# Attention with a mixture of experts: transposes by halves and the causal mask in the tiling of the scores

## The chip, the cores and the metric

The kernel runs on one core of a Trainium2 chip. The metric is the device time of one execution in microseconds. A core has TensorE (PE in the profile, its weight loads PEld), VectorE (DVE), ScalarE (ACT), GpSimd (POOL) and SyncE (SP, which here issues most DMAs). Each works through its own list of instructions in order, and semaphores tie them together.

## The reference

One layer on x of 8 x 1024 x 512 floats. Attention has 16 heads of 32 features. Queries, keys and values are no projections: each is the sine and cosine of an angle.

```python
theta_q = xh / (1.0 + jnp.abs(w_q)) + b_q + t * phi_q
Q = jnp.concatenate([cos_q, sin_q], axis=-1)          # K likewise
V = cos_v + sin_v
scores = jnp.einsum('bqhd,bkhd->bhqk', Q, K) / scale
scores = jnp.where(causal, -jnp.inf, scores)          # keys after the query
attn = jax.nn.softmax(scores, axis=-1)
out = jnp.einsum('bhqk,bkhd->bqhd', attn, V).reshape(B, S, D)
theta_out = out / (1.0 + jnp.abs(w_out)) + b_out       # then cos + sin
```

Then x = x + attention(layernorm(x)), and x = x + ffn(layernorm(x)). The ffn is a mixture of 8 experts, two for each token, each expert with room for 160 tokens of a sequence; an expert is 512 to 2048 to 512 with a relu.

## The kernel before

The attention comes first, up to about 1476 us, then the experts. All of it is in fp32.

Attention goes through 32 steps n, one for each sequence b and chunk c of four heads (128 features). Four heads are two pairs pr; the two heads of a pair lie in partitions 0 to 63 and 64 to 127 of a qk tile, cosine and sine together being 64 features. The index a is the head within a pair.

scores (L574) computes, for a pair and a half h of 512 queries, blocks of 128 keys against the queries that may see them. Each score tile holds two PSUM banks, one for each head. The two matmuls of a block use 64 rows of the array each ("64*128" in the profile), and run side by side. Half 0 has three tiles (512 columns; 384 + 128; 256), half 1 seven (five of 512; 384 + 128; 256). A profile line counts an fp32 matmul twice, since it is two passes. ScalarE takes Exp of a tile into an e tile in SBUF (L580). In the three tiles of each half that hold blocks on the diagonal, VectorE multiplies the diagonal blocks by seen, a matrix of ones and zeros (L590). attend (L604) multiplies e by the values: 128 rows, 64 columns for each head ("128*64"), all blocks added in one PSUM bank av. VectorE takes av out to av_sb with a factor (L611). turn transposes av_sb in four 128 x 128 transposes (L641, "128*128"), and VectorE divides by the sum that came along as a 33rd value (L644, L646).

qk_pre does the transposes of the normalized input for the next but one step (L458, then L463 on VectorE), eight for a step. qk_abs, square, sine and qk_sin are ScalarE's part of sine and cosine (L474, L399, L402, L482). qk_post multiplies on VectorE (L405) and rearranges through eight DMAs. v_pre, v_post make the values, o_pre, o_post the output angle. ScalarE loads a table before the sines and another before the next Exp.

The router of sequence b - 1 begins at the end of step c = 0 of the next sequence: statistics and a root on VectorE, then for each tile of 128 tokens rows (L679, normalized, sent off by DMA), features (four transposes, L691, and a copy, L692), parts (L698, "128*32") and whole (L710). Later parts choose experts and places.

The order on TensorE, VectorE and ScalarE is written out by hand, as the program emits it. Generators yield after each tile; run goes round its generators, two tiles each in turn, and steps the asides (qk_abs, v_pre, layernorm1, the router) after each turn. So score tiles and products alternate in short runs:

```python
av11, e01 = run(
    attend(n - 1, 1, 1, e11) if late else iter(()), scores(pairs[0], 1),
    aside=asides,
)
```

[...] ps_sc has two score tiles (four banks), ps_av two, ps_tr two of one bank for all transposes and the router's matmuls. In the experts' stage ps_p takes the six that the first two held.

Of the kernel before, what the change touches and what calls it, by code (L numbers as in the profile page):

```python
# [11 lines left out]
F32 = mybir.dt.float32  # L12
# [54 lines left out]

ROOT_GUESS = float(0x5F3759DF)
# [3 lines left out]
def preln_attn_moe_kernel(  # L72
# [61 lines left out]
    avp = to_router.pool("avp", 2, **left)  # L134
# [52 lines left out]
    ps_tr = to_end.pool("ps_tr", 2, space=PSUM)  # L187
# [12 lines left out]
    ps = ps_tr.tile([P, 6 * NCH], F32, name="ps_t")  # L200
# [24 lines left out]
    seen = own.tile([P, P], F32, name="seen")  # L225
# [17 lines left out]

    def rest_of_loads():

        for op, t in ((ALU.is_ge, seen), (ALU.is_gt, before)):
            nc.gpsimd.affine_select(
                out=t, in_=ones, compare_op=op, fill=0.0, base=0, pattern=[[1, P]],
                channel_multiplier=-1,
            )  # L250
        nc.gpsimd.iota(
# [48 lines left out]
    ps_sc = to_pairs.pool("ps_sc", 2, space=PSUM)  # L300
# [27 lines left out]
    def load_b1():  # L328
        t = own.tile([E * NHC, P], F32, name="vec_in")
        nc.sync.dma_start(t, b1.rearrange("e (c p) -> (e c) p", p=P))  # L330
        ps = ps_tr.tile([P, P], F32, name="ps_t")
# [7 lines left out]
    def load_mid(b):  # L339
# [6 lines left out]
        st = small.tile([P, NTT, NCH, nc.vector.BN_STATS_DIM], F32, name="st_mid")  # L346
# [101 lines left out]
    def qk_pre(n):  # L448
# [5 lines left out]
        for h in range(2):  # L454
            yield
            ps = ps_tr.tile([P, 4, P], F32, name="ps_t")
            for t in range(4):
                nc.tensor.transpose(  # L458
                    ps[:, t, :], xn_tiles[b][h][:, t, c * P : (c + 1) * P], ident
                )  # L460
            for i in range(2):
                cols = (slice(None), i, slice(512 * h, 512 * (h + 1)))
                nc.vector.scalar_tensor_tensor(  # L463
                    p[cols], ps.rearrange("p t q -> p (t q)"),
                    inv_qk[:, i * NCH + c : i * NCH + c + 1], base[cols], ALU.mult, ALU.add,
                )
        yield p, r
# [97 lines left out]
    def scores(pair, h):  # L565

        es = []
        for parts in tiles_of(h):
            n = sum(w for _, _, w, _ in parts)
            ps = ps_sc.tile([P, 2, 512], F32, name="ps_s")  # L570
            for kb, q0, w, at in parts:
                for a in range(2):
# [3 lines left out]
                        rhs=pair[r, 0, q0 : q0 + w], start=True, stop=True,  # L576
                    )

# [4 lines left out]
            if parts[0][0] >= 4 * h:  # L583

                if len(parts) == 1:
                    own_keys, k = e[:, :, :P], seen.unsqueeze(1).to_broadcast([P, 2, P])
# [7 lines left out]
    def attend(n, pr, h, es):  # L594
# [4 lines left out]
        for i, parts in enumerate(tiles):  # L599
            if i:  # L600
                yield
# [12 lines left out]
    def run(*gens, aside=()):  # L614
# [3 lines left out]
        while live:  # L618
            for i in list(live):
# [7 lines left out]
                for g in aside:  # L627
                    next(g, None)
# [666 lines left out]
```

## Time and profile before

| | |
|---|---|
| median of 3 runs | 3486.86 us (3486.4 to 3488.84) |
| the profiled execution | 3486.65 us, span 3484.9 us |
| TensorE busy | 3302.9 us (95%) |
| VectorE busy | 2469.3 us (71%) |
| ScalarE busy | 1315.7 us (38%) |
| granted TensorE clock | 0.992 |

The span runs from the first to the last instruction of the profiled execution. Matmul starts are recorded, their ends are modelled, so busy time of TensorE overlaps between neighbours, and a gap between two runs is read from start to start. In the groups a line names the code line, engine, operation and tiles, then its count, busy time, mean duration in ns, and the idle time of the engine before it with what ended it. x3072 of L574 is 1536 matmuls of two passes.

### The profile page before, as it was taken

The page shows a single profiled execution, that of the slowest core. Times are in us where ns is not written, and L with a number is a line of the kernel's source. Part 1 is how long each engine was busy: PE and PEld are TensorE (multiplying, and loading weights), DVE is VectorE, ACT ScalarE, POOL GpSimd, SP SyncE. Part 2 cuts the span into 40 slices and gives each one's busy share as a digit, 9 for nine tenths or more (in the row PEclk, how much of TensorE's full clock was granted, in tenths as well). Part 3 has the DMA queues.
Part 4 walks back from the last instruction along what each step waited for, and adds up shares of the span by engine and source line. Part 5 has one row for each costly group of instructions (what it writes and reads, how often), then busy time and mean ns, then how long its engine had stood idle before and what let it go on. Part 6 is the DMA issues. An engine that isn't in the chain of part 4 may idle for free.

```text
span 3484.9 us, 43387 instructions
## 1 busy us (share of the span) xinstructions
PE 3302.9 (95%) x15974; PEld 2171.9 (62%) x15974; DVE 2469.3 (71%) x5569; ACT 1315.7 (38%) x1609; POOL 391.1 (11%) x346
## 2 busy tenths in 40 slices
PE   3899999999999999889999999999999999999998
PEld 1344444444444444458868868778778688688687
DVE  7897989898989878574684585576566747746844
ACT  5676767676767676420120111111111101101201
POOL 0000202020202020232101101100110111011010
PEclk9999999999999999999999999999999999999999
DMA  4434343434353434142232322422322323322321
GB/s 142 125 93 148 90 154 91 154 91 153 91 178 89 132 87 135 46 137 39 75 106 46 112 61 49 112 55 61 106 46 67 103 43 76 103 38 76 105 40 25
DMA packets 242684, 320.45 MB, mean 92 GB/s; under 512 B 30312, under 2 KB 163112, under 8 KB 230056
## 3 DMA queue, kind: packets, MB, share of 16 engines
q1 hardware_dynamic: 220304, 275.54, 26.7%
q0 software_dynamic: 22080, 42.10, 6.8%
q8 instruction: 127, 2.08, 0.2%
q14 instruction: 85, 0.70, 0.1%
q10 hardware_dynamic: 88, 0.02, 0.0%
HBM read 188.67 MB, written 61.82 MB: 72 GB/s over the span
## 4 chain that ended last, share of the span: by engine, by line
PE 79%; DVE 12%; ACT 5%; issue 2%; DMA 1%; POOL 0%; POOLq 0%; DVEq 0%; ACTq 0%; SPq 0%
PE ps_p L1010 27%; PE ps_p L965 24%; PE av L604 11%; PE ps_s L574 11%; ACT e L580 4%; PE ps_t L641 2%; DVE e L590 1%; PE ps_t L921 1%; PE ps_t L458 1%; PE ps_t L691 1%; DVE qk_c L405 1%; DVE av_sb L611 1%; DVE qk_r L405 1%; DVE xn L679 0%; PE ps_t L698 0%
## 5 line engine op out<-in xcount | busy, mean ns | idle before, releaser
L580 ACT ACTIVATE e<-ps_s 128x1024 f32<-128x1024 f32 (+1 forms) x640 | 564.5, 937 | 389.8 <-PE ps_s L574 385.9
L574 PE MATMUL ps_s<-qk 64*128 64x512 f32 (+3 forms) x3072 | 607.7, 512 | 62.0 <-ACT e L580 40.4
L1010 PE MATMUL ps_p<-w,hid 128*128 128x256 f32 x2560 | 569.4, 380 | 0.0
L604 PE MATMUL av<-e,v 128*64 128x512 f32 (+3 forms) x3072 | 557.4, 499 | 5.8 <-DVE e L590 5.8
L1010 PEld LDWEIGHTS ps_p<-w,hid 128*128 128x128 f32 x2560 | 484.5, 190 | 66.3
L574 PEld LDWEIGHTS ps_s<-qk 64*128 64x128 f32 x3072 | 277.9, 187 | 326.1 <-issue 160.2
L1010 PE MATMUL ps_p<-w_t,hid 128*128 128x256 f32 x1920 | 430.5, 379 | 1.3 <-DVE w_t L886 1.3
L604 PEld LDWEIGHTS av<-e,v 128*64 128x64 f32 x3072 | 195.5, 138 | 322.1 <-issue 264.2
L1010 PEld LDWEIGHTS ps_p<-w_t,hid 128*128 128x128 f32 x1920 | 361.7, 190 | 49.7 <-DVE w_t L886 2.1
L965 PE MATMUL ps_p<-xe_s,t 128*128 128x256 f32 (+1 forms) x1024 | 299.8, 436 | 3.4 <-DVE t L950 3.4
L965 PE MATMUL ps_p<-xe,w 128*128 128x256 f32 (+1 forms) x1024 | 298.3, 434 | 0.2
L965 PE MATMUL ps_p<-xe,t 128*128 128x256 f32 (+1 forms) x1024 | 296.8, 433 | 0.0
L657 POOL DMA_INDIRECT slot_d<-token,slot x128 | 149.4, 1167 | 1146.9 <-issue 636.9
L590 DVE TENSOR_TENSOR e<-e,seen 128x256 f32<-128x256 f32 (+1 forms) x384 | 184.4, 510 | 118.3 <-ACT e L580 115.1
L965 PEld LDWEIGHTS ps_p<-xe_s,t 128*128 128x128 f32 x1024 | 194.6, 191 | 87.3 <-DVE t L950 7.9
L1039 ACT COPY p<-ps_p 128x256 f32<-128x256 f32 x40 | 14.7, 368 | 612.5 <-PE ps_p L1010 612.5
L965 PEld LDWEIGHTS ps_p<-xe,t 128*128 128x128 f32 x1024 | 194.4, 190 | 80.5
L965 PEld LDWEIGHTS ps_p<-xe,w 128*128 128x128 f32 x1024 | 192.8, 190 | 82.5 <-DVE hid L983 5.9
L1032 POOL DMA_INDIRECT out_dram<-y,slots x80 | 126.4, 1580 | 671.5 <-DVE y L1027 528.6
L914 POOL DMA_INDIRECT xg<-xn_d,source x80 | 78.3, 979 | 1026.8 <-PE ps_t L921 1017.1
L922 DVE COPY xe<-ps_t 128x512 f32<-128x512 f32 x80 | 55.3, 691 | 194.9 <-PE ps_t L921 194.3
L980 ACT ACTIVATE p<-ps_p,b_t 128x256 f32<-128x256 f32 (+1 forms) x128 | 65.5, 512 | 330.5 <-DVE y L1026 170.0
(193 smaller groups left out, 3874.0 us busy)
## 6 DMA issues: line engine op xcount, KB each, us to landing
w<-in_L_ffn_W_dram SPq DMA_DIRECT2D x256, 256.0 KB, 3.2
qk<-qk_c SPq DMA_DIRECT2D x128, 256.0 KB, 4.5
qk<-qk_r SPq DMA_DIRECT2D x128, 256.0 KB, 4.6
w<-in_L_ffn_W_dram SPq DMA_DIRECT2D x64, 512.0 KB, 7.1
qk_base<-base_d SPq DMA_DIRECT2D x29, 1024.0 KB, 5.1
xn_d<-xn SPq DMA_DIRECT2D x72, 256.0 KB, 2.0
x_mid<-in_L_attn_x_dram SPq DMA_DIRECT2D x16, 1024.0 KB, 8.5
out_dram<-x_mid SPq DMA_DIRECT2D x8, 2048.0 KB, 11.7
```

The lines of the kernel that those rows point to most:

```text
L405: nc.vector.scalar_tensor_tensor(out, f.bitcast(F32), LIFT, s, ALU.add, ALU.mult)
L574: nc.tensor.matmul(ps[:, a, at : at + w], lhsT=pair[r, 1, kb * P : (kb + 1) * P], rhs=pair[r, 0, q0 : q0 + w], start=True, stop=True,)
L580: nc.scalar.activation(e, ps[:, :, :n], AF.Exp, scale=UNIT * UNIT / math.sqrt(2 * DH))
L590: nc.vector.tensor_tensor(own_keys, own_keys, k, ALU.mult)
L604: nc.tensor.matmul(av[a * 64 : (a + 1) * 64, q0 - 512 * h :], lhsT=vt[:, kb, 2 * pr + a, :], rhs=es[i][:, a, at : at + w], start=kb == 0, ...
L641: nc.tensor.transpose(ps[:, t, :], av_sb[:, t * P : (t + 1) * P], ident)
L657: nc.gpsimd.indirect_dma_start(out=slot_d[b], out_offset=bass.IndirectOffsetOnAxis(ap=idx, axis=0), in_=src, in_offset=None,)
L914: nc.gpsimd.indirect_dma_start(out=xg, out_offset=None, in_=xn2_d[i % 2], in_offset=bass.IndirectOffsetOnAxis(ap=source[:, e, j0 + j, None ...
L965: nc.tensor.matmul(ps, lhsT=weights[:, k, :], rhs=rows[:, k, :], start=k == 0, stop=k == 1)
L980: nc.scalar.activation(p1, product(b11, a11), AF.Identity, bias=b1_t[:, e * NHC + q : e * NHC + q + 1])
L1010: nc.tensor.matmul(ps, lhsT=hs[k][:, part, cols], rhs=ws[k][weight], start=k == 0, stop=k == NHQ - 1,)
L1032: nc.gpsimd.indirect_dma_start(out=out, out_offset=bass.IndirectOffsetOnAxis(ap=meta[:, e, jj[r], 0:1], axis=0), in_=ys[r], in_offset=None ...
```

## The change

Transposes go by halves: by_halves transposes the upper and the lower 64 rows of a block apart, each into one bank of a tile, in the tiling of the scores. The tiles come from ps_sc, which now has three of two banks; ps_tr is gone until the experts' stage. qk_pre, turn and features each fill one such tile with eight blocks, and VectorE reads it with other strides. turn is called once for both halves of a pair.

The mask is added to the scores before Exp: bf16 matmuls of keys_b (an identity, shifted by part) with later_b (0 or -FAR) add onto the diagonal blocks, four for each of those tiles. VectorE's multiplication is gone.

The order is new. some steps generators a given number of tiles; a step goes in runs of three to five tiles of scores or products, with transposes next to scores; the ten score tiles of a pair follow each other, both halves in one list. The router's rows and features come in twos. The e tiles keep their number; avp has three buffers.

```diff
+FAR = 1000.0 * math.sqrt(2 * DH) / (UNIT * UNIT)
...
+    ps_sc = to_pairs.pool("ps_sc", 3, space=PSUM)
+    def two_banks():
+        return ps_sc.tile([P, 2, 512], F32, name="ps_s")
+    def by_halves(turned, src):
+        for a in range(2):
+            r = slice(a * 64, (a + 1) * 64)
+            nc.tensor.transpose(turned[:, a, :], src[r, :], ident[r, r])
...
-    seen = own.tile([P, P], F32, name="seen")
+    keys_b = own.tile([P, 2, P], BF16, name="keys_b")
+    nc.vector.memset(keys_b, 0.0)
+    later_b = own.tile([P, 2, P], BF16, name="later_b")
...
+    later = row2.tile([P, NCH, 2 * P], F32, name="xT", bufs=1)[:, :3, :P]
+    def mask():
+        for part in range(2):
+            for a in range(2):
+                r = slice(a * 64, (a + 1) * 64)
+                nc.vector.tensor_copy(later_b[r, part, :], later[r, 1 + part - a, :])
+                nc.vector.tensor_copy(keys_b[r, part, part * 64 : part * 64 + 64], ident[r, r])
...
-        for h in range(2):
-            yield
-            ps = ps_tr.tile([P, 4, P], F32, name="ps_t")
-            for t in range(4):
-                nc.tensor.transpose(
-                    ps[:, t, :], xn_tiles[b][h][:, t, c * P : (c + 1) * P], ident
+        ps = two_banks()
+        for t in range(NTT):
+            by_halves(
+                ps[:, :, t * 64 : (t + 1) * 64],
+                xn_tiles[b][t // 4][:, t % 4, c * P : (c + 1) * P],
+            )
+        for i in range(2):
+            for a in range(2):
+                cols = lambda t: t[:, i, :].rearrange("p (t a q) -> p t a q", a=2, q=64)[:, :, a, :]
+                nc.vector.scalar_tensor_tensor(
+                    cols(p), ps[:, a, :].rearrange("p (t q) -> p t q", q=64),
+                    inv_qk[:, i * NCH + c : i * NCH + c + 1], cols(base), ALU.mult, ALU.add,
                 )
-            for i in range(2):
-                cols = (slice(None), i, slice(512 * h, 512 * (h + 1)))
-                nc.vector.scalar_tensor_tensor(
-                    p[cols], ps.rearrange("p t q -> p (t q)"),
-                    inv_qk[:, i * NCH + c : i * NCH + c + 1], base[cols], ALU.mult, ALU.add,
-                )
-        yield p, r
+            yield p, r
...
-    def scores(pair, h):
-        es = []
+    def scores(pair, h, es):
         for parts in tiles_of(h):
             n = sum(w for _, _, w, _ in parts)
-            ps = ps_sc.tile([P, 2, 512], F32, name="ps_s")
+            ps = two_banks()
+            own_keys = parts[0][0] >= 4 * h
             for kb, q0, w, at in parts:
                 for a in range(2):
                     r = slice(a * 64, (a + 1) * 64)
                     nc.tensor.matmul(
                         ps[:, a, at : at + w], lhsT=pair[r, 1, kb * P : (kb + 1) * P],
-                        rhs=pair[r, 0, q0 : q0 + w], start=True, stop=True,
+                        rhs=pair[r, 0, q0 : q0 + w], start=at == 0, stop=not own_keys,
+                        skip_group_check=True,
                     )
+            if own_keys:
+                for part, w in ((0, 64), (1, P)):
+                    for a in range(2):
+                        r = slice(a * 64, (a + 1) * 64)
+                        out_, late = ps[:, a, :w], later_b[r, part, :w]
+                        if len(parts) == 2:
+                            out_ = ps[:, a, :].rearrange("p (k q) -> p k q", q=P)[:, ::3, :w]
+                            late = late.unsqueeze(1).to_broadcast([64, 2, w])
+                        nc.tensor.matmul(
+                            out_, lhsT=keys_b[r, part, :], rhs=late,
+                            start=False, stop=part == 1, skip_group_check=True,
+                        )
             e = ep.tile([P, 2, n], F32, name=f"e_{n}", bufs=8 if n == 512 else 2)
             nc.scalar.activation(
                 e, ps[:, :, :n], AF.Exp, scale=UNIT * UNIT / math.sqrt(2 * DH)
             )
-            if parts[0][0] >= 4 * h:
-                if len(parts) == 1:
-                    own_keys, k = e[:, :, :P], seen.unsqueeze(1).to_broadcast([P, 2, P])
-                else:
-                    own_keys = e.rearrange("p a (k q) -> p a k q", q=P)[:, :, ::3, :]
-                    k = seen.unsqueeze(1).unsqueeze(1).to_broadcast([P, 2, 2, P])
-                nc.vector.tensor_tensor(own_keys, own_keys, k, ALU.mult)
             es.append(e)
-            yield es
-    def attend(n, pr, h, es):
+            yield
+    def attend(n, pr, h, es, halves):
         vt = v_tiles[n % 2]
         av = ps_av.tile([P, 512], F32, name="av")
         tiles = tiles_of(h)
         for i, parts in enumerate(tiles):
-            if i:
-                yield
             for kb, q0, w, at in parts:
                 for a in range(2):
                     nc.tensor.matmul(
...
+            if i + 1 == len(tiles):
+                av_sb = avp.tile([P, 512], F32, name="av_sb")
+                q = 2 * (n % NCH) + pr
+                nc.vector.tensor_scalar(av_sb, av, inv_o[:, q : q + 1], None, ALU.mult)
+                halves.append(av_sb)
+            yield
+    def some(count, *gens):
+        for gen in gens:
+            while count and next(gen, 0) is None:
+                count -= 1
...
-    def turn(pr, h, av_sb, p):
-        ps = ps_tr.tile([P, 4, P], F32, name="ps_t")
-        for t in range(4):
-            nc.tensor.transpose(ps[:, t, :], av_sb[:, t * P : (t + 1) * P], ident)
-        av = ps.rearrange("p t (a f) -> p t a f", a=2)
-        rec = small.tile([P, 4, 2, 1], F32, name="rec")
+    def turn(pr, halves, p):
+        ps = two_banks()
+        for t in range(NTT):
+            by_halves(
+                ps[:, :, t * 64 : (t + 1) * 64],
+                halves[t // 4][:, t % 4 * P : (t % 4 + 1) * P],
+            )
+        av = ps.rearrange("p a (t f) -> p t a f", f=64)
+        rec = small.tile([P, NTT, 2, 1], F32, name="rec")
         nc.vector.reciprocal(rec, av[:, :, :, DH : DH + 1])
         dst = p.rearrange("p (t a d) -> p t a d", a=HPC, d=DH)
         nc.vector.tensor_tensor(
-            dst[:, 4 * h : 4 * h + 4, 2 * pr : 2 * pr + 2, :], av[:, :, :, :DH],
-            rec.to_broadcast([P, 4, 2, DH]), ALU.mult,
+            dst[:, :, 2 * pr : 2 * pr + 2, :], av[:, :, :, :DH],
+            rec.to_broadcast([P, NTT, 2, DH]), ALU.mult,
...
+        def features(xns):
+            xT = row2.tile([P, NCH, 2 * P], F32, name="xT", bufs=1)
+            if b == B - 1:
+                for i, xn in enumerate(xns):
+                    ps = pools["ps_tr"].tile([P, NCH, P], F32, name="ps_t")
+                    for c in range(NCH):
+                        nc.tensor.transpose(ps[:, c, :], xn[:, c * P : (c + 1) * P], ident)
+                    copy(xT[:, :, i * P : (i + 1) * P], ps)
+                    yield xT
+            else:
+                ps = two_banks()
+                for i, xn in enumerate(xns):
+                    for c in range(NCH):
+                        at = (NCH * i + c) * 64
+                        by_halves(ps[:, :, at : at + 64], xn[:, c * P : (c + 1) * P])
+                for a in range(2):
+                    copy(
+                        xT.rearrange("p c (i a q) -> p i c a q", a=2, q=64)[:, :, :, a, :],
+                        ps[:, a, :].rearrange("p (i c q) -> p i c q", i=2, q=64),
+                    )
+                yield xT
...
-        ahead = rows(0)
+        ahead = [rows(0), rows(1)]
         yield "tiles"
-        lg, xT_ = None, None
+        lg, xT = None, None
         for g in range(NTT // 2):
             if g:
-                lg = parts(xT_)
-            xT_ = row2.tile([P, NCH, 2 * P], F32, name="xT", bufs=1)
-            for i in range(2):
-                xn = ahead
-                if 2 * g + i + 1 < NTT:
-                    ahead = rows(2 * g + i + 1)
-                features(xn, xT_, i)
-                if i == 0:
-                    yield
+                lg = parts(xT)
+            for xT in features(ahead):
+                yield
+            if g + 1 < NTT // 2:
+                ahead = [rows(2 * g + 2), rows(2 * g + 3)]
             if g:
                 whole(g - 1, lg)
             yield
         yield "sums"
-        lg = parts(xT_)
+        lg = parts(xT)
...
+    mask()
...
+        es, halves = [[], []], [[], []]
+        products = [attend(n, 0, h, es[h], halves[0]) for h in range(2)]
+        if late:
+            products.insert(0, attend(n - 1, 1, 1, e11, halves1))
+        ahead = [scores(pairs[0], h, es[h]) for h in range(2)]
+        places, v_box = [None], [None]
+        absolutes = keep(places, qk_abs(qk_st)) if more else iter(())
+        asides = [keep(v_box, v_pre(n + 1))] if more else [first_rows]
         if route is not None and c > 0:
             asides.append(part(route))
-        if not more:
-            asides.append(first_rows)
...
-        av11, e01 = run(
-            attend(n - 1, 1, 1, e11) if late else iter(()), scores(pairs[0], 1),
-            aside=asides,
-        )
+        def with_asides(count):
+            for _ in range(count):
+                some(1, *ahead)
+                for g in asides:
+                    next(g, None)
+        if late:
+            some(3, *products)
+        if n == 0:
+            with_asides(3)
+            qk_st = rest(qk_pre(1))
+            angle(*qk_st)
+            absolutes = keep(places, qk_abs(qk_st))
+            with_asides(2)
+        else:
+            with_asides(5)
+        some(2, absolutes)
+        if late:
+            some(3, *products)
+        with_asides(4)
+        some(2, absolutes)
+        some(3, *products)
+        with_asides(1)
+        rest(absolutes)
         for g in asides:
             rest(g)
+        if n == 1:
+            load_mid(0)
+        if late:
+            turn(1, halves1, pos)
+            o_st = o_pre(n - 1, pos)
...
+        some(NTT + 2, *products)
         if more:
             v_post(n + 1, v_st)
         if n == 0:
             load_base(2)
-        (e10,) = run(scores(pairs[1], 0))
-        turn(0, 1, av01, pos_n)
+        es, halves1 = [[], []], []
+        ahead = [scores(pairs[1], h, es[h]) for h in range(2)]
+        asides = []
+        if route is not None and c > 0:
+            asides.append(part(route))
+        with_asides(5)
+        turn(0, halves[0], pos_n)
         if late:
             square(o_st[0])
             o_post(n - 1, o_st)
-        places = [None]
-        asides = [keep(places, qk_pre(n + 2))] if n + 2 < NCK else []
-        if route is not None and c > 0:
-            asides.append(part(route))
-        e11, av10 = run(scores(pairs[1], 1), attend(n, 1, 0, e10), aside=asides)
+        some(3, attend(n, 1, 0, es[0], halves1))
+        with_asides(5)
+        if n + 2 < NCK:
+            qk_st = rest(qk_pre(n + 2))
...
+        last = (es[1], halves1, pos_n)
         pairs = next_pairs if more else None
-    turn(1, 0, av10, pos_n)
-    (av11,) = run(attend(NCK - 1, 1, 1, e11))
-    turn(1, 1, av11, pos_n)
+    rest(attend(NCK - 1, 1, 1, es[1], halves1))
+    turn(1, halves1, pos_n)
     to_pairs.close()
```

The hunks left out give parts, whole, places and the first gathers tiles from ps_sc in place of ps_tr (in the last sequence and in the experts' stage a new ps_tr serves), and build later on GpSimd.

## The prediction

> **What bounds the kernel now.** I read the page first (its busy times, then its costliest groups), then TensorE's timeline of one attention step, the list of waits between 100 and 1450 us, and ScalarE's timeline of the same step.
>
> From the page:
> ```profile
> PE 3302.9 (95%) x15974; PEld 2171.9 (62%) x15974; DVE 2469.3 (71%) x5569; ACT 1315.7 (38%) x1609; POOL 391.1 (11%) x346
> ...
> L580 ACT ACTIVATE e<-ps_s 128x1024 f32<-128x1024 f32 (+1 forms) x640 | 564.5, 937 | 389.8 <-PE ps_s L574 385.9
> ...
> L604 PE MATMUL av<-e,v 128*64 128x512 f32 (+3 forms) x3072 | 557.4, 499 | 5.8 <-DVE e L590 5.8
> ...
> L590 DVE TENSOR_TENSOR e<-e,seen 128x256 f32<-128x256 f32 (+1 forms) x384 | 184.4, 510 | 118.3 <-ACT e L580 115.1
> ```
> TensorE is the bound. The masking on VectorE (L590) keeps VectorE busy 184 us, yet TensorE waited for it 5.8 us in all (the idle column of L604): taking it away buys almost nothing on the path by itself.
>
> TensorE's timeline of an attention step without router work (start, duration, instructions, idle before):
> ```profile
> 728.57 5.81 PE L604 MATMUL av<-e,v 128*64 128x512 f32 x32
> 734.30 0.66 PE L641 MATMUL ps_t<-ident,av_sb 128*128 128x128 f32 x4
> 734.89 2.00 PE L574 MATMUL ps_s<-qk 64*128 64x512 f32 x12
> 737.17 0.70 PE L574 MATMUL ps_s<-qk 64*128 64x256 f32 x4 [0.28 <-ACT e L580]
> 737.80 0.66 PE L641 MATMUL ps_t<-ident,av_sb 128*128 128x128 f32 x4
> 738.39 1.99 PE L574 MATMUL ps_s<-qk 64*128 64x512 f32 x8
> 740.30 1.94 PE L604 MATMUL av<-e,v 128*64 128x512 f32 x12
> 742.18 0.66 PE L458 MATMUL ps_t<-ident,xn 128*128 128x128 f32 x4
> ```
> Starts are exact, ends are modelled, so I use starts. 3328 columns of L604 take 5.73 us (728.57 to 734.30), 1024 columns 1.88 (740.30 to 742.18): 1.67 ns a column plus **0.16 us for each run**. Scores of 1024 columns take 1.91 (738.39 to 740.30): 0.20 us a run. Four transposes take 0.59: 0.11 each, and 0.15 for the run. So each change of tiling (64*128, 128*64, 128*128) costs 0.15 to 0.20 us that the busy time hides. Such a step holds 22 runs and lasts 39.6 us (712.41 to 752.03, turn to turn).
>
> Who waits:
> ```profile
> PE ps_s L574 <- ACT e L580: 32.6, 123, 0.3
> ...
> PE ps_t L691 <- DVE xn L679: 15.7, 14, 1.2
> ...
> PE ps_t L698 <- DVE xT L692: 12.0, 14, 1.5
> ```
> The 0.2 to 0.3 us waits recur four times a step: two score tiles are all that PSUM has room for, and the third waits for Exp. The router's waits for VectorE come in one step of four.
>
> The view of av_sb gives the attention's length:
> ```profile
> L611 DVE TENSOR_SCALAR av_sb<-av,inv_o x128: 730/743/752, 78.1 to 1468.8; 128x512 f32<-128x512 f32 x128
> ```
> 127 intervals of 10.95 us, so 43.8 us for each of 32 steps, 1402 us in all. **Ledger before:** scores and products 32 x 18,432 columns x 1.67 ns = 985; 1016 transposes x 0.1075 = 109; router matmuls about 27; 793 runs in the order (254 of scores x 0.20, 539 x 0.16) = 137. Sum 1258, so 144 us are waits.
>
> **What the Trainium skill says.** "TensorEngine Tiling (Array Packing)", Key Properties: changing the tiling mode drains TensorE, changing the tile within a mode doesn't. The trace agrees: 0.15 to 0.20 us at each change, none inside a run. Same page, Gotcha 1: different row tiles must write different PSUM banks; that is why a tile of halves needs two banks. "TensorE: Matmul & The Clock Gate", LDWEIGHTS: columns / 1.2 ns whatever the rows, 107 ns for 128 columns; the trace's 0.11 us for each fp32 transpose agrees. Same page, Weight-path perf modes: 128 non-fp32 weights load about twice as fast; the trace has no bf16 matmul, so nothing here shows it.
>
> **The change, part by part.**
>
> *Runs.* The order of TensorE's instructions has 447 runs instead of 793 (223 in the 64*128 tiling, 224 others): 223 x 0.20 + 224 x 0.16 = 80. Gain **57 us**.
>
> *Transposes by halves.* 1016 transposes become 1016 pairs. A half loads 64x128 weights and streams 64 columns. The two loads are in different rows and go side by side; next load beside this stream: 107 ns a pair, as before, **0**. If load and stream don't overlap it is 107 + 53 = 160 ns: +53. I take 0.
>
> *Masks.* 384 score tiles get four bf16 loads and four matmuls (64 and 128 columns, twice that in the two-block tiles). The first pair of loads hides behind the scores; the second load and the next fp32 load show: 54 + 107 to 107 + 107 ns. I take 0.19 us: **+73**. Lower end 0.12 (+46). The trace before doesn't show bf16 between fp32; if that costs as much as a tiling change on the way in and out, 0.5 (+192).
>
> *VectorE.* 184 us of L590 go; two divisions of 256 elements become one of 512. Worth the 5.8 us above, counted with the waits. The eight small copies of mask() and POOL's extra memset and select fall into a prologue that waits for qk (51.6 us): under 1 us.
>
> *PSUM.* ps_tr's two banks go to ps_sc, now three tiles; transposes take turns in them. The four waits of a step go: PE needs the fourth tile only when Exp of the first is done. But the order stacks ScalarE's work:
> ```profile
> 727.41 1.28 ACT L482 ACT_TABLE_LOAD   x1
> 728.70 2.00 ACT L482 ACTIVATE qk_c<-qk_c,quarter_c 128x2048 f32<-128x2048 f32 x1
> 730.62 1.89 ACT L402 ACTIVATE qk_r<-qk_r 128x2048 f32<-128x2048 int32 x1
> 732.41 1.99 ACT L402 ACTIVATE t_r<-t_r 128x1024 f32<-128x1024 int32 x2
> 734.42 1.28 ACT L580 ACT_TABLE_LOAD   x1
> ```
> This block of 8.3 us lies beside turn and the products (0.9 + 6.1 us on TensorE). Now ten Exp, not seven, stand before it. Walking one step through from the end of the qk transposes before it, with Exp starts 0.92 us apart (two in 1.94 us on ScalarE's timeline, each lasting 1.02): Exp of the last tile at 17.7 us, block done at 27.0, first score tile of the second half ready at 25.4, fourth tile held to 28.0 instead of 27.1: about 1.0 us a step, with residue 1.2; 25 steps without router tiles, 30 us.
>
> *Router.* features now comes after three products and one score tile, 4 us after the end of the qk transposes. On VectorE stand ahead of its xn: L463 (2.7), the shift (1.2), bn_aggr (1.1), the root (2.9), two rows (1.0): 9 us. TensorE waits 4.7 (before 1.2), and some 1.7 more at the next pair: 6.4 x 7 = 45. All score tiles and products behind it wait too. The last step's wait for gathers stays, about 10. Of the DMAs, rows of two tiles now issue together (four in SP's queue in place of two at a time) and load_mid(0) moves behind the first half of step 1; its data is needed a step later. No other DMA is moved past a queue that ends a wait above: 0.
>
> *Sum.* Waits 144 to 85 (-59), runs -57, masks +73: **-43**. The profiled execution took 3486.65 (span 3484.9, 1.75 around it), 0.2 under the median of the three. So 3444. The experts' stage, from about 1476 us, keeps its instructions.
>
> **The rivals.**
> 1. *bf16 among fp32 is dear (slower).* The place is the end of each of the 384 masked tiles. At 0.30 us a tile the gain is gone (0.19 + 43/384); at 0.35 the sum is 384 x 0.16 - 43 = +18: 3505. At the 0.5 of above it would be 3563, a tail that I leave out. For it: nothing of the kind runs in the trace. Against: a transpose and an ordinary matmul follow one another in one tiling without a gap.
> 2. *The waits only move (slower).* Transposes and scores share three tiles and VectorE reads in order, so score tiles wait for VectorE instead of Exp. Waits stay 144: -57 + 73 = +16: 3503. For it: VectorE is 86% busy between 420 and 1084 us (572 of 664). Against: 184 of some 1200 us go, 15%.
> 3. *Masks are cheap and waits small (faster).* 0.12 us and 50 us of waits: -57 + 46 - 94 = -105: 3382.
> 4. *Halves don't overlap their loads.* 3444 + 53 = 3497, slower.
>
> **How the numbers follow.** Forecast 0.5, rival 1 0.15, rival 2 0.12, rival 3 0.16, rival 4 0.07. Its own range is 3416 to 3472; with the others 3380 to 3520. A measurement here tells 0.2% (7 us) from no change. Faster: 0.45 of the forecast and 0.15 of rival 3, 0.60; same 0.09; slower 0.31.
>
> **What would show it.** Runs of scores from start to next start: a masked tile 0.15 to 0.21 us longer than its columns. No start-to-start loss between a transpose by halves and scores. L604 waiting for nothing. The fourth tile of the second half waiting for Exp about 1 us. In one step of four, transposes of xn waiting for VectorE some 5 us. I am wrong if a masked tile costs over 0.30 us, if a pair of halves costs over 0.13, or if score tiles wait for VectorE outside the router's step.

## The result and the profile after

The changed kernel takes 3507.47 us (3505.37 to 3508.05, four runs) against 3486.76 us before in the same comparison: ratio 1.0057, 95% interval 1.004 to 1.0074. It is 21 us slower where 43 us less were forecast. 3507 lies inside the range, on the other side of zero.

The page of the changed kernel, its busy times and two of its groups (instructions, then busy us, mean ns, then idle before them and what ended it):

```profile
PE 3279.3 (94%) x18522; PEld 2209.2 (63%) x18522; DVE 2300.8 (66%) x5064; ACT 1318.7 (38%) x1609; POOL 394.5 (11%) x349
...
L626 ACT ACTIVATE e<-ps_s 128x1024 f32<-128x1024 f32 (+1 forms) x640 | 568.5, 939 | 406.6 <-PE ps_s L620 216.5
...
L640 PE MATMUL av<-e,v 128*64 128x512 f32 (+3 forms) x3072 | 535.1, 494 | 0.0
```

The products (L640, formerly L604) wait for nothing, VectorE has lost 169 us and TensorE is busy 24 us less, in a span 19 us longer. So TensorE gained waits. The same view of av_sb as before says where the time is not:

```profile
L648 DVE TENSOR_SCALAR av_sb<-av,inv_o x128: 731/742/752, 69.2 to 1479.5; 128x512 f32<-128x512 f32 x128
```

It now starts 9 us earlier (69.2, was 78.1) and ends 11 us later. From the first expert matmul on (at 1482 us here, at 1470 before) it takes 7 us more (2022 against 2015). TensorE's timeline of a step without router tiles, and of its end (start, duration, instructions, idle before):

```profile
592.06 1.13 PE L606 MATMUL ps_s<-qk 64*128 64x512 f32 x4
593.02 0.25 PE L620 MATMUL ps_s<-later_b,keys_b 64*128 64x64 bf16 x4
593.11 1.09 PE L606 MATMUL ps_s<-qk 64*128 64x384 f32 x8
594.03 0.33 PE L620 MATMUL ps_s<-later_b,keys_b 64*128 64x128 bf16 x4
594.19 0.60 PE L606 MATMUL ps_s<-qk 64*128 64x256 f32 x4
594.63 0.25 PE L620 MATMUL ps_s<-later_b,keys_b 64*128 64x64 bf16 x4
596.59 2.04 PE L606 MATMUL ps_s<-qk 64*128 64x512 f32 x8 [1.71 <-ACT e L626]
...
605.73 0.66 PE L202 MATMUL ps_s<-ident,xn 64*128 64x64 f32 x16
606.32 2.79 PE L640 MATMUL av<-e,v 128*64 128x512 f32 x12
```

Here the edits do what they should. The two-block masked tile lasts from 593.11 to 594.19, 0.23 more than its columns; tiles of one block lose about 0.1. The eight pairs of half transposes last 0.59 with the change of tiling behind them, 0.06 a pair. The fourth tile waits 1.7 us for Exp. From one cosine activation to the next, such a step takes 37.9 us (before 39.6), or 38.8 (before 40.8). The router's step (c = 1) takes 57.9, and took 50.5. Its timeline:

```profile
610.01 0.25 PE L620 MATMUL ps_s<-later_b,keys_b 64*128 64x64 bf16 x4
615.06 1.12 PE L202 MATMUL ps_s<-ident,xn 64*128 64x64 f32 x16 [4.80 <-DVE xn L710]
615.94 2.05 PE L606 MATMUL ps_s<-qk 64*128 64x384 f32 x8
617.75 0.56 PE L620 MATMUL ps_s<-later_b,keys_b 64*128 64x128 bf16 x4
618.07 1.09 PE L606 MATMUL ps_s<-qk 64*128 64x256 f32 x4
...
622.12 1.01 PE L202 MATMUL ps_s<-ident,xn 64*128 64x64 f32 x16 [1.79 <-DVE xn L710]
...
652.25 1.00 PE L763 MATMUL ps_s<-gather_e,lg 128*128 128x8 f32 x4 [2.90 <-DVE lg L756]
...
654.35 3.73 PE L606 MATMUL ps_s<-qk 64*128 64x512 f32 x8
657.87 0.90 PE L202 MATMUL ps_s<-ident,av_sb 64*128 64x64 f32 x16
```

Three waits stand in it. What follows the first and the third is new: the two-block tile (384 columns and 128) takes 2.05 where it takes 1.09 above, the two 512-column tiles 3.73 instead of 2.04. The windows of these stretches carry the granted clock in the column after POOL:

```profile
615.00:623.00 8.00, 6.07 (x62) 4.09 (x62) 5.38 (x9) 1.61 (x2) 0.00 (x0) 0.63 0.81 315
624.00:632.00 8.00, 7.70 (x60) 3.74 (x60) 4.53 (x11) 4.81 (x5) 0.00 (x0) 1.00 0.46 158
652.00:659.00 7.00, 6.75 (x38) 4.06 (x40) 0.47 (x3) 2.49 (x3) 0.00 (x0) 0.54 0.73 178
662.00:669.00 7.00, 7.00 (x64) 3.54 (x62) 5.89 (x15) 4.37 (x5) 0.00 (x0) 1.00 0.01 2
```

After such a wait TensorE runs at half its clock for some us. Over the kernel the mean granted clock falls from 0.992 to 0.971; (1 - clock) x span is the most that half clock can have cost: 28 us before, 102 after. That counts idle time too. TensorE was busy at half clock for 150 us here and for 37 before, which is 57 us more of lost TensorE time. The Trainium skill, "TensorE: Matmul & The Clock Gate", HAM oscillation, states the rule: idle gaps of TensorE over about 3.4 us halve its clock, and the work behind them starts cold. The trace agrees for the 4.8 us wait, and shows more: the 2.9 us wait was followed by half clock too. The prediction didn't use that section.

The traces also show when a wait counts. All stretches of half clock begin on a grid of 3.41 us and last whole multiples of it. Cut along this grid from 100 us on, the traces of all 13 kernels here agree: a piece at full clock in which TensorE was idle over 60% of the time was always followed by half clock, a piece idle under 34% never; in between both occur. So the share of one piece that waits fill decides, and not the length of a wait alone.

VectorE's timeline shows why xn is late:

```profile
609.19 1.23 DVE L426 TENSOR_SCALAR qk_r<-qk_f 128x2048 int32<-128x2048 int32 x1
610.34 1.11 DVE L700 BATCH_NORM_AGGREGATE mv<-st_mid 128x2 f32<-128x24 f32 x8
...
614.37 1.00 DVE L710 TENSOR_SCALAR xn<-x_mid,mv,rstd 128x512 f32<-128x512 f32 x2
...
621.43 1.18 DVE L710 TENSOR_SCALAR xn<-x_mid,mv,rstd 128x512 f32<-128x512 f32 x2 [2.53 <-DMA xn_d<-xn]
```

The root stands between the angles and xn, as forecast; the second pair of rows waits for the stores of the first, since both buffers of xn hold rows on their way out. The first wait is 4.8 us in all seven steps with router tiles, the second 1.7 to 3.3.

### The profile page after: what moved, and what is told of

It reads as the page before. It is cut to its first block, busy times and chain, and to the rows that moved or that the text cites. A ratio compares the mean times of both kernels' runs of the same rounds, so it can differ in the third digit from the quotient of the medians.

```text
span 3503.7 us, 48081 instructions
## 1 busy us (share of the span) xinstructions
PE 3279.3 (94%) x18522; PEld 2209.2 (63%) x18522; DVE 2300.8 (66%) x5064; ACT 1318.7 (38%) x1609; POOL 394.5 (11%) x349
## 4 chain that ended last, share of the span: by engine, by line
PE 72%; ACT 13%; DVE 8%; DMA 4%; issue 2%; POOL 0%; POOLq 0%; ACTq 0%; DVEq 0%; SPq 0%
PE ps_p L1069 27%; PE ps_p L1024 24%; PE ps_s L606 11%; PE av L640 7%; ACT e L626 4%; ACT qk_c L514 2%; ACT qk_f L430 2%; PE ps_s L202 2%; DMA xn_d<-xn 2%; DMA slot_d<-token,slot 1%; ACT t_r L433 1%; ACT qk_r L433 1%; ACT L514 1%; ACT v_p L430 1%; PE ps_t L980 1%
## 5 line engine op out<-in xcount | busy, mean ns | idle before, releaser
L606 PE MATMUL ps_s<-qk 64*128 64x512 f32 (+3 forms) x3072 | 640.6, 534 | 63.5 <-ACT e L626 40.4
L640 PE MATMUL av<-e,v 128*64 128x512 f32 (+3 forms) x3072 | 535.1, 494 | 0.0
L640 PEld LDWEIGHTS av<-e,v 128*64 128x64 f32 x3072 | 203.1, 138 | 289.8 <-issue 272.8
L963 POOL DMA_INDIRECT xg<-xn_d,source x80 | 78.1, 976 | 1026.9 <-PE ps_t L980 1020.4
L1043 ACT ACTIVATE hid<-hid 128x256 f32<-128x256 f32 (+1 forms) x128 | 60.1, 470 | 319.2 <-DVE hid L1042 319.2
L1056 ACT ACTIVATE hid<-hid,b_more 128x256 f32<-128x256 f32 (+1 forms) x128 | 71.8, 561 | 271.5 <-DVE hid L1055 271.5
```

Of the source, the lines that this page charges most:

```text
L606: nc.tensor.matmul(ps[:, a, at : at + w], lhsT=pair[r, 1, kb * P : (kb + 1) * P], rhs=pair[r, 0, q0 : q0 + w], start=at == 0, stop=not own ...
L640: nc.tensor.matmul(av[a * 64 : (a + 1) * 64, q0 - 512 * h :], lhsT=vt[:, kb, 2 * pr + a, :], rhs=es[i][:, a, at : at + w], start=kb == 0, ...
L963: nc.gpsimd.indirect_dma_start(out=xg, out_offset=None, in_=xn2_d[i % 2], in_offset=bass.IndirectOffsetOnAxis(ap=source[:, e, j0 + j, None ...
L1056: nc.scalar.activation(h12, h12, AF.Relu, bias=more)
```

## The experiments

The first theory: the order of the router's step makes TensorE wait, and each long wait is paid again in half clock. The rivals: the masks on TensorE or the transposes by halves cost more than they save.

**1. Work in the waits.** Same order; fp32 matmuls of no use stand where TensorE waited for xn and lg.

```diff
+        def keep_busy(ps, count, rows=2):
+            for _ in range(count):
+                for a in range(rows):
+                    r = slice(a * 64, (a + 1) * 64)
+                    nc.tensor.matmul(ps[:, a, :], lhsT=ident[r, :], rhs=inv_v[r, :], start=True, stop=True)
...
+                keep_busy(ps, 3)
...
-            for xT in features(ahead):
+            for xT in features(ahead, (5, 2, 0, 0)[g]):
```

> The changed kernel with extra matmuls (identity times a constant tile, in the tiling of the scores, overwritten afterwards) put in front of the router's first two groups of transposes (five and two pairs of 512 columns) and of its last logits (three single ones), in seven of eight sequences. Nothing is computed differently. They fill the waits of 5.0, 2.2 and 3.1 us with 8.6 us of TensorE work for each sequence. Theory 'clock': the waits leave TensorE idle long enough for the granted clock to fall to a half for 3 to 7 us each time, and that (133 us more at half clock than before, some 60 us lost) is what the sum had left out. Then it gets FASTER with more work, by 25 to 55 us (3450 to 3482), and the granted clock goes from 0.971 to over 0.98. Theory 'waits alone': the clock is an effect without weight; then 3505 to 3520.

Measured: 3486.04, ratio to before 0.9991 (0.9983 to 1.0), clock 0.989. TensorE is given more to do and the kernel is 21 us faster than without it: half clock is a cost of its own. The gain is less than hoped: (1 - clock) x span fell by 64 us, 102 to 38. Part of the half clock lay over time in which TensorE would have waited anyway: its work at half clock fell from 150 to 46 us, worth 52. And the filler, ten rounds of 0.85 us a router step (the last three are pairs too, not single ones as expected), overran: the waits were 4.8, 1.8 and 2.9, and 0.4, 0.4, 1.6 and 1.5 of waits still stand between, so some 3 us a step, 20 in all, were added. About 11 us of the difference stay open.

**2. The mask back on VectorE**, in the new order.

```diff
-            if own_keys:
-                for part, w in ((0, 64), (1, P)):
...
+            if own_keys:
...
+                nc.vector.tensor_tensor(own, own, k, ALU.mult)
```

> The changed kernel with the mask back on VectorE (Exp, then the product with ones and zeros) and no bf16 matmul; order and transposes stay. Theory 'masks cheap': a masked tile shows 0.09 us (single block) to 0.2 us (two blocks) in the trace, 50 us of TensorE over 384 tiles, while VectorE gets 190 us back, in a step where TensorE waits for VectorE. Then the two about cancel: 3485 to 3530. Theory 'masks are the loss': bf16 between fp32 costs over 0.3 us a tile; then it is 70 us or more faster, under 3440.

Measured: 3547.86, ratio 1.0162 (1.0145 to 1.0179), clock 0.957: 40 us slower than the changed kernel, worse than the range. TensorE's waits between 100 and 1500 us:

```profile
PE ps_s L202 <- DVE xn L690: 63.6, 15, 6.0
PE ps_s L202 <- DVE av_sb L628: 51.0, 15, 8.9
```

The second line was 6.9 in the changed kernel, the first 53.0. With the mask on VectorE the transposes of av_sb wait for it, and none of these waits lies in the router's step. This is near rival 2 of the prediction, but the waits stand at transposes; score tiles don't wait for VectorE here either. Work at half clock grew too, from 150 to 228 us.

**3. Whole transposes**, in the new order.

```diff
-            by_halves(ps[:, :, t * 64 : (t + 1) * 64], halves[t // 4][...])
+            whole_block(ps, t, halves[t // 4][...])
```

> The changed kernel with whole 128-row transposes in place of halves, into the same two-bank tiles and in the same order. Theory 'halves pay': a pair of halves takes 0.06 us against 0.11 for a whole transpose (1016 of them, 46 us), and each block of transposes next to scores adds a change of tiling (some 26 us). Then slower by 30 to 75 us: 3537 to 3582. Theory 'halves are the loss' (loads don't overlap): faster by 30 to 50 us.

Measured: 3528.53, ratio 1.0113 (1.0096 to 1.013), clock 0.979. Halves save 21 us, less than expected. Between 100 and 1450 us TensorE waits 90 us for xn, lg and Exp here, and 109 in the changed kernel; its work at half clock is 109 us here and 150 there, worth 21. So most of what the shorter transposes gain is waited away for the same VectorE and ScalarE, and the longer waits are paid again in half clock.

**4. The masks alone.** The kernel before, its order, its whole transposes, two score tiles; only the mask is done by the bf16 matmuls.

```diff
+            if own_keys:
+                for part, w in ((0, 64), (1, P)):
...
-            if parts[0][0] >= 4 * h:
...
-                nc.vector.tensor_tensor(own_keys, own_keys, k, ALU.mult)
```

> The kernel before, in its own order of TensorE, with its whole transposes and two score tiles; only the mask is changed: bf16 matmuls in the score tiles instead of VectorE's multiplication. Mask theory (0.13 us a masked tile, as the starts in the changed kernel show): 384 x 0.13 = +50, the 5.8 us of waits for VectorE gone, a part of the 33 us of waits for Exp hidden under the mask matmuls: 3505 to 3530, granted clock still 0.99. Rival (bf16 among fp32 is dear, 0.30 us or more): +109 or more, 3590 and up. If VectorE's 184 us were on the path in places that its waits do not show: 3487 or less.

Measured: 3468.73, ratio 0.9944 (0.9927 to 0.9961), clock 0.993: under the range, 19 us faster than before. The third case of the expectation held. TensorE's waits between 100 and 1450 us:

```profile
PE ps_s L593 <- ACT e L613: 10.3, 31, 1.4
PE ps_t L735 <- DVE lg L728: 5.7, 7, 0.8
PE ps_t L723 <- DVE xT L717: 4.5, 7, 1.1
```

Its waits for VectorE are 10 us; before, the four lines for xn, xT, av_sb and lg had 44. Those for Exp went from 32.6 to 10.3. The router's step fell from 50.5 to 47.6 us while plain steps rose from 39.6 to 40.5 and from 40.8 to 41.1. Of VectorE's work only L590 is gone, so L590 had been on the path as what stood ahead of others in VectorE's queue.

So the chain closes: before 3487; masks 3469; new order 3529 (experiment 3); halves 3507. **The new order costs 60 us**, the two other edits gain 39. "Order" here takes in the three shared score tiles and one turn for both halves, which no run separates. The steps don't simply add: the mask's move is worth 18 in the old order and 40 in the new one (experiment 2).

**5. The router later.** In the router's step seven products come ahead, and the router's first part begins with the third score tile.

```diff
+        tiles_first = route is not None and c == 1
-            some(3, *products)
+            some(7 if tiles_first else 3, *products)
+        if tiles_first:
+            with_asides(2)
+            asides.append(part(route))
+            with_asides(3)
```

> The changed kernel with one thing moved, in the seven steps with router tiles: seven tiles of products in place of three open the step, and the router's transposes are stepped from the third score tile on, not from the first. The work is the same. Theory 'order': the loss is that TensorE comes to the router's rows 5.0 us before VectorE has them (and 2.2 us again at the next pair). Then both waits fall under 1.5 us, one or two of three clock dips go with them, and the router step goes from 57 to 48-51 us: 3430 to 3470. Rival 'shared tiles': VectorE just cannot keep up with transposes in the three shared tiles, and the waits come back later in the step: 3495 to 3510.

Measured: 3475.03, ratio 0.9965 (0.995 to 0.9979), a little above the range; 32 us less than the changed kernel. The work is the same; only its order within seven steps differs. What waits remain, on TensorE's timeline:

```profile
610.84 0.64 PE L751 MATMUL ps_s<-xT,wr_sb 128*32 128x256 f32 x8 [2.90 <-DVE xT L736]
613.50 1.33 PE L202 MATMUL ps_s<-ident,xn 64*128 64x64 f32 x16 [2.02 <-DVE xn L710]
...
642.14 0.94 PE L763 MATMUL ps_s<-gather_e,lg 128*128 128x8 f32 x4 [4.56 <-DVE lg L756]
```

**6. The sums later too.** The last of the three waits is for lg; its part of the router moves to the last five score tiles.

```diff
-        if route is not None and c > 0:
+        if route is not None and c > 1:
...
         some(3, attend(n, 1, 0, es[0], halves1))
+        if route is not None and c == 1:
+            asides.append(part(route))
```

> The kernel of the late tiles, and in the router's step the sums (parts and whole) stepped among the last five score tiles of the step in place of the first five of its second half. Order theory (in the late tiles' trace the sums wait 4.7 us for lg behind VectorE's sine products, and 3.4 to 6.8 us of half clock follow): 7 x (4.7 + 1.7 to 3.4) = 45 to 57 less, some of it given back at the qk transposes that now stand behind the sums: 3425 to 3455, clock 0.98 or more. Rival (the wait only moves to the qk transposes and the clock still falls): 3465 to 3480.

Measured: 3491.46, ratio 1.0009 (1.0001 to 1.0018): a miss, 16 us slower than experiment 5.

```profile
647.25 3.17 PE L606 MATMUL ps_s<-qk 64*128 64x512 f32 x8 [4.03 <-ACT e L626]
...
657.84 0.70 PE L763 MATMUL ps_s<-gather_e,lg 128*128 128x8 f32 x4 [1.53 <-DVE lg L756]
```

In the old place the wait for lg had covered another: the fourth tile's for Exp behind the sines. With lg gone, Exp holds TensorE 4.0 us, with half clock behind it, and lg holds it again further down. Between 100 and 1450 us the waits for Exp grew from 36.1 to 64.4 and those for lg fell from 31.9 to 9.2; work at half clock grew from 112 to 123 us, worth 5. That makes some 11 of the 16 us; the rest stays open.

**7. Products between the router's pairs.** On top of 6, the first half's three products move between the first two pairs of row tiles, and one score tile goes without a router step.

```diff
-            with_asides(3)
+            with_asides(2)
+            some(3, *products)
+            held = asides.pop()
+            with_asides(1)
+            asides.append(held)
```

> The kernel with the late sums, and in the router's step the three products of the first half moved between the first and the second pair of the router's row tiles, one score tile stepped without the router. Order theory: of the 2.9 and 2.0 us that TensorE waited there for xT and xn some 3 go, and with a wait under 2 us the half clock after it goes as well (6.8 us of it, worth 3.4): 7 x 3 to 6.4 = 21 to 45 less than the late sums. Rival (VectorE's wait for the stores of xn holds it all the same): within 10 us of the late sums.

Measured: 3442.58, ratio 0.9867 (0.9851 to 0.9884), clock 0.983. 49 us less than experiment 6, a little over the range; the router's step takes 47.8 us.

```profile
604.59 2.37 PE L640 MATMUL av<-e,v 128*64 128x512 f32 x16
...
608.81 0.64 PE L751 MATMUL ps_s<-xT,wr_sb 128*32 128x256 f32 x8
610.53 1.01 PE L202 MATMUL ps_s<-ident,xn 64*128 64x64 f32 x16 [1.09 <-DVE xn L710]
...
632.42 2.05 PE L606 MATMUL ps_s<-qk 64*128 64x512 f32 x8 [2.79 <-ACT e L626]
```

The wait for xT is gone, xn's is 1.1, and Exp's is 2.8 instead of 4.0. In this sequence full clock stands behind it (two tiles in 2.05); behind the same wait of 2.79 us in the six others half clock began, at once or up to 1.4 us later. All in all, work at half clock fell from 123 to 83 us.

**8. Score tiles ahead of the products** in the other steps, so that ScalarE starts earlier.

```diff
+        early = 2 if late and not tiles_first else 0
+        with_asides(early)
         if late:
...
-            with_asides(5)
+            with_asides(5 - early)
```

> The kernel of the held products, and in every step without the router's tiles the first two score tiles stand ahead of the first three products, so that ScalarE starts on them 2 to 3 us earlier and its block of sines ends earlier. If the 1.7 us wait of the fourth tile of the second half is ScalarE's order alone: 24 steps x 1.5 to 1.7 = 36 to 41 less, two changes of tiling more in each (24 x 0.36 = 9): 25 to 35 us less than the held products. Rival (ScalarE's block waits for something else, the sine arguments from VectorE or e tiles): 5 to 10 us more than the held products.

Measured: 3468.06, ratio 0.9948 (0.9931 to 0.9964): 25 us slower than experiment 7, more than either theory said. The wait is untouched:

```profile
718.32 2.04 PE L606 MATMUL ps_s<-qk 64*128 64x512 f32 x8 [1.72 <-ACT e L626]
```

ScalarE stood idle 2.4 us in the middle instead, and the sines still began 2 us after TensorE's last tile of the half. Plain steps grew by 0.4 to 0.5 us, some 11 in all. Three of the router's steps took 51 us or more where one did in experiment 7; the seven together took some 6 us more. The rest stays open.

**9 to 11. ScalarE's order, the sums behind their wait, and both.** The scalar order (on top of 8) fills ScalarE's idle time and moves the half's last score tile ahead of the last three products. The later sums (on top of 7) leave more work between parts and whole.

```diff
+        if early:
+            some(2, absolutes)
...
+        if early:
+            with_asides(1)
         some(2, absolutes)
         some(3, *products)
-        with_asides(1)
+        if not early:
+            with_asides(1)
```

```diff
+            with_asides(2)
             asides.append(part(route))
-        with_asides(5)
+            with_asides(1)
+            held = asides.pop()
+            with_asides(2)
+            asides.append(held)
```

> The kernel of the early tiles; in every step without the router's tiles ScalarE takes the two absolutes right behind the first two tiles (it stands idle 2.4 us there) and the two squares behind the fifth, and the last score tile of the first half goes ahead of the last three products. In the early tiles' trace the sines still began 2 us after TensorE's last tile of the first half, so the wait of 1.5 to 1.7 us was untouched. If that tile's place sets it, the block starts some 2 us earlier and the wait goes: 24 x 1.5 = 36 less than the early tiles, 3425 to 3440. Rival (the arguments of the sines come late from VectorE, so that an earlier place only makes Exp wait): 3455 to 3475.

> The kernel of the held products; in the router's step the last sum's first half (parts) goes behind the third of the last five score tiles and its second (whole) behind the qk transposes, since lg comes 3.7 us after parts there. Order theory: the 2.0 us wait for lg goes, 7 x 2 = 14, and with it some of the half clock after it (3.4 us, worth 1.7): 10 to 25 less than the held products, 3417 to 3433. Rival (VectorE's chain is late at the next place too, the transposes of av_sb or xn): within 7 us of the held products.

> Both: the scalar order and the later sums. If both theories hold they add up: 10 to 25 less than the scalar order, and the fastest of all only if ScalarE's wait was worth more than the 0.45 us a step that the early tiles cost: 3405 to 3425. If ScalarE's rival holds, 3440 to 3465.

| kernel | us | ratio to before, 95% interval | clock | step c = 0 | c = 1 | c = 2 | c = 3 |
|---|---|---|---|---|---|---|---|
| before | 3486.76 | | 0.992 | 39.6 | 50.5 | 42.8 | 40.8 |
| changed | 3507.47 | 1.0057 (1.004 to 1.0074) | 0.971 | 37.9 | 57.9 | 43.3 | 38.8 |
| held products (7) | 3442.58 | 0.9867 (0.9851 to 0.9884) | 0.983 | 37.9 | 47.8 | 43.0 | 38.8 |
| scalar order (9) | 3407.34 | 0.9769 (0.9753 to 0.9786) | 0.988 | 36.5 | 46.9 | 41.5 | 38.3 |
| later sums (10) | 3432.84 | 0.9846 (0.9829 to 0.9862) | 0.987 | 37.9 | 48.0 | 40.8 | 38.8 |
| both (11) | 3396.35 | 0.9737 (0.9721 to 0.9753) | 0.989 | 36.5 | 46.9 | 40.4 | 38.3 |

The steps are medians over the sequences of their traces, from one cosine activation to the next, so the effects at a step's end fall into the next one. The scalar order gave 61 us against experiment 8, over its range: the waits for Exp between 100 and 1450 us fell by the 36 expected (59.8 to 23.8), and work at half clock from 86 to 51 us, worth 18 more. The later sums gave 10 against experiment 7, at the lower end, with intervals that overlap; on top of the scalar order they gave 11, and there no two runs overlap. Both together beat every other kernel here, 2.6% under before, and 9 us under their range. ScalarE's timeline in it:

```profile
662.02 2.00 ACT L506 ACTIVATE qk_c<-qk_r 128x1024 f32<-128x1024 int32 x2 [0.41 <-DVE qk_r L426]
...
669.60 4.59 ACT L626 ACTIVATE e<-ps_s 128x1024 f32<-128x1024 f32 x5 [0.64 <-PE ps_s L606]
674.09 1.14 ACT L430 ACTIVATE v_p<-v_p,split_c 128x1024 f32<-128x1024 uint16 x1
675.24 1.28 ACT L514 ACT_TABLE_LOAD   x1
```

Of the squares only that of the values (the 1.14 us) still stands between the half's last Exp and the table of the sines. TensorE's waits for Exp are 22.7 us between 100 and 1400 us; they were 54.8 in experiment 7.

## Why the prediction was wrong

Experiments 3 and 4 divide the sum. The new order was to gain 116 us (runs 57, waits 59) and cost 60. The masks were to cost 73 and gained 18. The halves were to give 0 and gained 21. So the step that failed is the waits in the new order, 144 to 85. In the prediction's own ledger the attention now has 985 + 61 for transposes + 27 + 55 for masks + 80 for runs (as forecast), 1208 us, and by the intervals of av_sb (11.10 us) it lasts 1421: 213 us are waits and half clock, not 85. Of these the waits view of the changed kernel lists about 133, and TensorE's 130 us of work at half clock in the attention cost 65; some 15 stay open.

- **The clock, left out.** This is the largest part of the step that failed: the sum priced every wait once and put half clock at nothing, without a reason. The wait of 4.7 us that I had seen coming in each router step halves the clock, and so does the one for lg that I had not. That is up to 74 us (102 - 28), or 57 if only TensorE's work at half clock is counted. At that size it turns the sign. Experiment 1 shows that at least 21 of them are real; more of it comes back in 5 and 7 together with waits, and cannot be split from them there.
- **Router, +45.** 4.80 us at xn was forecast as 4.7: right, with the right work on VectorE ahead of it. The second wait, forecast as 1.7, is 1.7 to 3.3, and all waits for xn are 53 us. The second is for the stores of xn, where I had put the DMAs at 0. And the wait for lg at the start of the second half, 2.9 us in each of seven steps, 20 us in the waits view, was missed: lg stands behind the sine products on VectorE.
- **Masks, +73.** Starts give about 0.1, 0.23 and 0.1 for the three masked tiles of a half, 0.14 in the mean: 384 x 0.14 = 55. Rival 1 falls.
- **VectorE's relief, -5.8 and counted with the waits.** Mis-sized. In the old order the masks' move is worth -18 although TensorE pays about 55 for it: some 57 us of waits went (44 to 10 for VectorE, 33 to 10 for Exp). The two make -2; what the other 16 were stays open. I read the idle column of the group that VectorE's mask feeds, and not what is queued behind the mask. It also means that most of the waits that the order was to remove go with the mask alone.
- **Transposes by halves, 0.** Mis-sized: 0.06 us a pair against 0.11, for 1016 pairs about -50; experiment 3 shows -21, after the waits and the clock that it loses. Rival 4 falls. The Trainium skill, "TensorE: Matmul & The Clock Gate", LDWEIGHTS, gives the same time whatever the rows, and the sum took that time for a pair; the trace of the changed kernel shows a pair of half loads with its streams in 0.06 us, one whole in 0.11.
- **ScalarE's block, 1.0 us a step.** The mechanism was right: the fourth tile waits, for Exp behind the sines. It measured 1.5 to 1.7; 35 us in the attention against the 30 of the sum. Experiments 8 and 9 show what sets it: the place of the half's last score tile and the squares behind it.
- **Runs, -57.** No run changes the number of runs alone. In the step from experiment 4 to 3 a plain step falls from 40.5 to 39.0 and from 41.1 to 39.8, the new wait for Exp already paid, so the term (1.8 us a step) is not contradicted; its size stays open.
- **Rivals 2 and 3.** Rival 2 names 3503, four under the result, by luck: score tiles didn't wait for VectorE outside the router's step, and masks and halves cost less than its sum has. Of rival 3 the cheap masks came true (0.14, it has 0.12), the small waits didn't.
- **The signs.** None of the three signs of being wrong appeared: a masked tile cost 0.14 us, a pair of halves 0.06, and score tiles waited for VectorE 0.6 us in all. They watched prices of single instructions, and the clock was not among them.
- **The experts' stage, no change.** It took 7 us more, 5 of them at one place, a gather of GpSimd's that TensorE waited 3.67 us for before (TensorE's timeline):

```profile
1618.96 1.09 PE L980 MATMUL ps_t<-ident,xg 128*128 128x128 f32 x4 [8.87 <-DMA xg<-xn_d,source]
```

  GpSimd issues it behind its scatters to slot_d. The first of these waits for VectorE's token until 1552 us here and until 1532 before, and the last begins at 1602, before at 1580. No run tests what delays them.

## What to carry to other kernels

On TensorE a wait of some 3 us can have a second price: look for stretches of double durations behind it, and for a mean clock that falls, before summing. Making TensorE's list shorter can lengthen its waits for the engines that it doesn't shorten (experiment 3: 90 to 109 us), so the place of the slowest helper's work in the new order decides: reordering seven steps (experiments 5 to 7) was worth 65 us here, the two edits 39. And an engine that is seldom waited for by name can still hold the path, through what stands in its queue behind the work that one takes away.

## What the runs showed of the hardware

- Half clock came after waits of 4.8, 4.0 and 2.9 us and lasted 3.41 us or a multiple of it (3.4 to 17 in the attention of the changed kernel). A wait of 2.79 us in experiment 7 had half clock behind it in six sequences of seven. One of 1.5 us at 694 us of the changed kernel had it too (two tiles in 2.91): with other gaps it left TensorE idle 48% of the piece of the 3.41 us grid that ended at 695.98. In experiment 7 the wait that ended at 632.42 lay across two pieces, idle 29% and 53%, and full clock followed. No wait length decides; between an idle share of 34 and 60% of a piece both clocks follow.
- Two 64-row transposes side by side take 0.06 us, a whole 128-row one 0.11.
- bf16 matmuls between fp32 ones in one tiling cost about 0.1 us for four loads and four matmuls of 64 and 128 columns.
